# A gated delta-rule block with routed experts: the first stage written out in a fixed order of steps

## The chip, the cores and the metric

The kernel runs on one core of a Trainium2 chip. The metric is device time in microseconds (us). One core has a matrix engine (TensorE, called PE), a vector engine (VectorE, DVE), an activation engine (ScalarE, ACT), a general engine (GpSimd, POOL) and SyncE (SP), whose queue here issues nearly all DMA transfers. Each engine takes its own instructions in the order in which the program has them.

## The reference, cut to what matters

There are two sequences of 2048 tokens with 512 features each. They are normalised and go through 16 heads of a gated delta rule; the first 512 tokens go through 16 experts too (four for each token). All is 32-bit.

```python
xn = layernorm(x)                                   # (2, 2048, 512)
q, k, v = (silu(causal_conv4(xn @ W) + b) for ...)  # 16 heads of 128; k scaled by 128**-0.5
alpha, beta = sigmoid(xn @ Wa + ba), sigmoid(xn @ Wb + bb)
def step(S, (qt, kt, vt, at, bt)):                  # for each token, sequence and head
    err = S @ kt - vt
    S = at * S - bt * outer(err, kt)
    return S, S @ qt
o = layernorm(scan(step)) * ln_w + ln_b
attn = (o * sigmoid(xn @ Wg)) @ Wo
out = x + attn + experts(xn[:512], topk_idx, topk_weight, gate, up, down)
```

## The kernel before, in words

The tokens of a sequence are cut into 16 chunks of 128, four of which make a block of 512. Two heads make a unit; there are 16 units, eight for each sequence. Inside a chunk the recurrence is a set of matmuls with the inverse of a triangular 128x128 matrix; from chunk to chunk a state S is carried. Projections are done transposed (features on partitions, 512 tokens on the free axis), so that the convolution of four taps is three multiply-adds on DVE with shifted slices.

The program has two parts. The **recurrence** (`recurrence`) takes the units one after the other. Its order on PE, DVE, ACT and POOL is written out by hand: generators (`before`, `after`, `output`, `item`, `key_item`, `inverses`, `experts`) yield after each piece, and a loop steps them in turn. While it works on one block it computes the projections of the next block and the keys of the unit two ahead.

The **first stage** prepares what the recurrence needs at its start, and it is what the change touches. Its parts are:

- `norm(b)`, for both sequences: load x, mean and variance (L453, L454), 1/sqrt by a power on POOL (L458), scale (L467), transpose on PE (L473) and evict on ACT (L474), and matmuls with Wa and Wb (L476), 32 columns wide ("gate matmuls" below). Then come the decays: z, exp, log and cumulated sums over a chunk as matmuls with constant triangles (L513), transposed rows written to DRAM (a_d and gin_d). Sequence 0 stays in SBUF as xT; sequence 1 goes to DRAM (xT_d).
- `route`: the experts' lists, that is, which token goes to which tile of which expert (DVE, and small matmuls L938 to L944 and L1002, the latter with "place" matrices).
- `keys(u)` for units 0 and 1, eight pieces each (a block and a head): projection (L155), eviction to raw and cv on ACT (L132, L136), three taps on DVE (L141), SiLU (L146), scores (L205), the decay matrix by a scan on DVE over a row fetched from DRAM (L179 and L196; the row's buffer is single, so the next row is asked for after the scan), and their product (L209). The key, the decay and the product are saved to DRAM.
- `inverses(0)`: the inverses of the 32x32 diagonal blocks of unit 0 on POOL (L264, L267; 30 pairs of steps), written to DRAM as X_d.
- `projection(0)`: q, v and gate of the first block of unit 0, and the loads of its operands.

What sets the order there is a scheduler which takes the program's order and its own estimate of when each instruction is ready. Program order is norm(0), route, and then a loop: the keys of unit 0, all of `inverses(0)`, the keys of unit 1, with steps of norm(1) and of projection(0) put between them. The recurrence starts when all this is written down, and its first instructions can be moved ahead by the scheduler (two of its matmul lines are: L620 and L625 of the first chunk run near 250 us). The tiles of the inverses' operands (`ops` and `invs`) are made and zeroed after the stage.

PSUM banks are in four pools: ps_p (3), ps_l (2), ps_c (2) and ps_o (1).

```python
f0, p0, n1 = firsts(), projection(0), norm(1)
for i, _ in enumerate(f0):
    if i > 12:
        next(n1, None)
    if i in (20, 23, 26, 29):
        next(p0)
drain(n1)
```

Of the kernel before, what the change touches and what calls it, by code (L numbers as in the profile page):

```python
# [1 line left out]

# [5 lines left out]
F32 = mybir.dt.float32  # L8
I32 = mybir.dt.int32
AF = mybir.ActivationFunctionType  # L10
E = mybir.EngineType
# [32 lines left out]
def block_kernel(ctx, tc, x, wq, wk, wv, wg, wo, wa, wb, ba, bb, par, consts,  # L44
# [80 lines left out]
    def conv_taps(ps, p, h0, h, blk):  # L125
# [7 lines left out]
        if blk < NBK - 1:  # L133
            nc.gpsimd.tensor_copy(halo[p][h], raw[:, BLK:])
# [7 lines left out]

    def conv_silu(ps, p, h0, h, blk, dst):
        raw, cv = conv_taps(ps, p, h0, h, blk)
        conv_sum(raw, cv, p, h0 + h)
        nc.scalar.activation(dst, cv, AF.Silu)  # L146
# [73 lines left out]
    def keys(u, xts, bank_k=(ps_p, "p")):  # L220

        b, hp = divmod(u, NP)
        h0 = hp * HG
        begin_keys(u)  # L230
        for blk in range(NBK):
            for h in range(HG):
                ps = proj(wks[u], h, xts(b, blk))
                kt = ap.tile([P, BLK], F32, tag="kf", name="kf", bufs=2)
                conv_silu(ps, 1, h0, h, blk, kt)
                if (blk, h) == (NBK - 1, HG - 1):
                    load_wk(u + 1)
                nc.sync.dma_start(out=k_d[u][blk][h], in_=kt)
                yield
                pk = bank(*bank_k)  # L240
                scores(pk, kt)
                dec = dec_start(u, blk, h)
                tc.keep_in_program_order(dec_run(dec, u, blk, h))
                put_a(pk, dec, u, blk, h)
                yield
# [110 lines left out]
    def item(n, what, h):  # L356
# [20 lines left out]
        raw, cv = conv_taps(ps, p, h0, h, blk)  # L377
# [15 lines left out]
    def key_item(u, blk, h, xts):  # L393
# [15 lines left out]
        raw, cv = conv_taps(ps, 1, h0, h, blk)  # L409
# [19 lines left out]

    with ExitStack() as es:  # L430
        pre = es.enter_context(tc.tile_pool(name="pre", bufs=1))
        cstf = pre.tile([P, N_CONST * P + 1], F32, tag="cst", name="cst")
        nc.sync.dma_start(out=cstf, in_=consts[:, DW:])
        cst = cstf[:, 0:N_CONST * P].rearrange("p (n j) -> p n j", j=P)
# [6 lines left out]
        beta = [pre.tile([P, NC, H], F32, tag=f"beta{b}", name=f"beta{b}") for b in range(NB)]  # L441
        np_ = es.enter_context(tc.tile_pool(name="norm", bufs=2))
        def norm(b):
            psg = bank(ps_o, "o")
            for g in range(NBK):
                xin = [np_.tile([P, HID], F32, tag="xin", name="xin", bufs=4) for _ in range(CB)]
                for i in range(CB):
                    c = g * CB + i
                    nc.sync.dma_start(out=xin[i], in_=x[b, c * C:(c + 1) * C, :])
                mv = np_.tile([P, CB, 2], F32, tag="mv", name="mv")  # L450
                for i in range(CB):
                    st = np_.tile([P, 6], F32, tag="st", name="st")
                    nc.vector.bn_stats(st, xin[i])  # L453
                    nc.vector.bn_aggr(mv[:, i, :], st)  # L454
                ve = np_.tile([P, CB], F32, tag="ve", name="ve")
                nc.vector.tensor_scalar(ve, mv[:, :, 1], EPS, None, ALU.add)
                rs = np_.tile([P, CB], F32, tag="rs", name="rs")
                nc.gpsimd.tensor_tensor(rs, ve, mhalf[:, 0:CB], ALU.pow)  # L458
                if b == 0:
                    xt = xT[b, g] = xp.tile(  # L460
                        [P, NKT, BLK], F32, tag="xT", name=f"xT{b}_{g}", bufs=NBK)
                else:
                    xt = np_.tile([P, NKT, BLK], F32, tag="xt", name="xt", bufs=1)
                for i in range(CB):
# [4 lines left out]
                    if b == 0 and c < FC:  # L469
                        nc.sync.dma_start(out=xn_d[c * C:(c + 1) * C, :], in_=xn)  # L470
# [655 lines left out]
```

## Time and profile before

| | us |
|---|---|
| three runs | 3904.68, 3907.49, 3910.80 (median 3907.49) |
| the profiled execution, device time | 3906.37 |
| its span (first to last instruction) | 3904.3 |
| mean granted clock of TensorE | 0.98 |

| busy in the span | us |
|---|---|
| PE (matmuls; modelled ends) | 3770.2 |
| PEld (weight loads, beside matmuls) | 2461.4 |
| DVE | 2343.6 |
| ACT | 1701.5 |
| POOL | 1682.4 |

A line of the profile's tables of groups and waits names the line of the code, the engine, the tile written and the tiles read. A wait is put down to what released it last. "x8" in a timeline of PE counts records: a 32-bit matmul leaves two, so a projection (four matmuls over the 512 features) is x8. The granted clock is a share of TensorE's full speed.

### The profile page before, as it was taken

The page shows a single profiled execution, that of the slowest core. Times are in us where ns is not written, and L with a number is a line of the kernel's source. Part 1 is how long each engine was busy: PE and PEld are TensorE (multiplying, and loading weights), DVE is VectorE, ACT ScalarE, POOL GpSimd, SP SyncE. Part 2 cuts the span into 40 slices and gives each one's busy share as a digit, 9 for nine tenths or more (in the row PEclk, how much of TensorE's full clock was granted, in tenths as well). Part 3 has the DMA queues.
Part 4 walks back from the last instruction along what each step waited for, and adds up shares of the span by engine and source line. Part 5 has one row for each costly group of instructions (what it writes and reads, how often), then busy time and mean ns, then how long its engine had stood idle before and what let it go on. Part 6 is the DMA issues. An engine that isn't in the chain of part 4 may idle for free.

```text
span 3904.3 us, 59006 instructions
## 1 busy us (share of the span) xinstructions
PE 3770.2 (97%) x18046; PEld 2461.4 (63%) x18046; DVE 2343.6 (60%) x6132; ACT 1701.5 (44%) x4027; POOL 1682.4 (43%) x3046
## 2 busy tenths in 40 slices
PE   7769999999999999999999999999999999998899
PEld 6437767677677766666654466666666666664454
DVE  5536656666666667777750177777777777763231
ACT  3424444444444445555520055555555555542110
POOL 1236546465564636363630053636363545541010
PEclk7789999999999999999999999999999999999999
DMA  4634665655666553545573435353435444342322
GB/s 133 209 98 143 185 169 154 195 158 175 168 176 172 159 178 107 143 132 169 147 240 117 120 103 137 107 139 109 132 111 139 119 127 126 103 111 72 100 75 89
DMA packets 579705, 541.36 MB, mean 139 GB/s; under 512 B 354688, under 2 KB 421760, under 8 KB 574272
## 3 DMA queue, kind: packets, MB, share of 16 engines
q1 hardware_dynamic: 557280, 456.18, 40.6%
q0 software_dynamic: 22112, 81.41, 7.1%
q8 instruction: 147, 2.41, 0.3%
q14 instruction: 166, 1.36, 0.1%
HBM read 363.69 MB, written 173.67 MB: 138 GB/s over the span
## 4 chain that ended last, share of the span: by engine, by line
PE 85%; DVE 6%; DMA 4%; issue 2%; POOL 2%; SPq 1%; ACT 1%; POOLq 0%; DVEq 0%; ACTq 0%
PE p L155 39%; PE p L892 11%; PE p L1044 4%; DVE cv L141 3%; PE o L721 3%; PE l L625 3%; PE p L205 3%; PE o L724 3%; PE c L698 3%; PE c L707 3%; PE c L687 2%; PE p L1059 2%; PE l L640 1%; PE l L658 1%; PE l L667 1%
## 5 line engine op out<-in xcount | busy, mean ns | idle before, releaser
L141 DVE SCALAR_TENSOR_TENSOR cv<-raw,prm,cv 128x512 f32<-128x512 f32 x1152 | 909.5, 790 | 106.2 <-ACT cv L136 44.1
L892 PE MATMUL p<-wo,oTf 128*128 128x512 f32 x1024 | 459.7, 604 | 26.3 <-DMA oTf<-oT_d 25.1
L155 PE MATMUL p<-xT,wq 128*128 128x512 f32 x1024 | 484.6, 596 | 0.0
L653 POOL COPY inv<-iT 32x32 f32<-32x32 f32 x512 | 103.1, 201 | 884.4 <-DVE iT L645 685.1
L155 PE MATMUL p<-xT,wg 128*128 128x512 f32 x1024 | 482.0, 594 | 0.0
L155 PE MATMUL p<-xT,wv 128*128 128x512 f32 x1024 | 481.0, 593 | 0.0
L735 POOL TENSOR_TENSOR rs<-rs,mhalf 128x2 f32<-128x2 f32 x256 | 270.2, 1055 | 485.4 <-DVE rs L734 481.1
L132 ACT COPY raw<-p 128x512 f32<-128x512 f32 x384 | 223.4, 582 | 533.2 <-PE p L155 515.0
L155 PE MATMUL p<-xT,wk 128*128 128x512 f32 x896 | 433.5, 610 | 0.0
L702 ACT COPY w<-c 128x256 f32<-128x256 f32 x256 | 95.3, 372 | 635.0 <-PE c L698 635.0
L714 DVE SCALAR_TENSOR_TENSOR S<-S,gtot,c 128x128 f32<-128x128 f32 x480 | 145.2, 344 | 356.6 <-PE c L707 342.5
L892 PEld LDWEIGHTS p<-wo,oTf 128*128 128x128 f32 x1024 | 193.9, 194 | 252.2 <-issue 223.8
L267 POOL TENSOR_TENSOR Y<-Y,t 128x30 f32<-128x30 f32 (+14 forms) x480 | 308.4, 643 | 37.2
L136 ACT ACTIVATE cv<-p,prm 128x512 f32<-128x512 f32 x384 | 300.4, 782 | 1.7
L264 POOL TENSOR_TENSOR t<-Y 128x30 f32<-128x30 f32 (+14 forms) x480 | 286.2, 596 | 8.8 <-DMA Y<-aT_d 2.3
L155 PEld LDWEIGHTS p<-xT,wq 128*128 128x128 f32 x1024 | 178.0, 192 | 135.8 <-issue 135.8
L155 PEld LDWEIGHTS p<-xT,wg 128*128 128x128 f32 x1024 | 176.8, 191 | 132.3 <-issue 132.1
L155 PEld LDWEIGHTS p<-xT,wv 128*128 128x128 f32 x1024 | 176.3, 191 | 132.0 <-issue 132.0
L691 DVE SCALAR_TENSOR_TENSOR r<-c,gd,kv 128x128 f32<-128x128 f32 x480 | 145.3, 344 | 166.2 <-PE c L687 165.1
L155 PEld LDWEIGHTS p<-xT,wk 128*128 128x128 f32 x896 | 160.6, 198 | 126.3 <-issue 126.3
L388 POOL TENSOR_TENSOR qg<-q,gin 128x512 f32<-128x512 f32 x128 | 194.1, 1516 | 98.6 <-ACT q L386 98.6
L707 PEld LDWEIGHTS c<-w,kg 128*128 128x128 f32 x1024 | 154.1, 191 | 121.4 <-issue 102.1
(172 smaller groups left out, 7145.8 us busy)
## 6 DMA issues: line engine op xcount, KB each, us to landing
row<-a_d SPq DMA_DIRECT2D x128, 258.0 KB
dec_d<-decA SPq DMA_DIRECT2D x128, 258.0 KB
decB<-dec_d SPq DMA_DIRECT2D x64, 516.0 KB
k_d<-kf SPq DMA_DIRECT2D x128, 256.0 KB
k<-k_d SPq DMA_DIRECT2D x64, 512.0 KB
gin<-gin_d SPq DMA_DIRECT2D x128, 256.0 KB
aT_d<-aTf SPq DMA_DIRECT2D x128, 256.0 KB
oT_d<-oT SPq DMA_DIRECT2D x256, 128.0 KB
```

Source lines behind the costliest of these rows:

```text
L132: nc.scalar.copy(raw[:, KS - 1:], ps)
L136: nc.scalar.activation(cv, ps, AF.Identity, bias=cbias(p, h0 + h), scale=tap(p, h0 + h, KS - 1))
L141: nc.vector.scalar_tensor_tensor(cv, raw[:, j:j + BLK], tap(p, h, j), cv, ALU.mult, ALU.add)
L155: nc.tensor.matmul(ps, lhsT=w[:, k, h * D:(h + 1) * D], rhs=xt[k], start=(k == 0), stop=(k == NKT - 1))
L264: nc.gpsimd.tensor_tensor(t, bass.AP(col.tensor, col.offset, [col.ap[0], (Q, j), (0, n)]), bass.AP(row.tensor, row.offset, [row.ap[0], (0, ...
L267: nc.gpsimd.tensor_tensor(Y[:, 0:j, j + 1:], Y[:, 0:j, j + 1:], t, ALU.add)
L388: nc.gpsimd.tensor_tensor(qg[:, h, :], qt[:, h, :], gin, ALU.mult)
L691: nc.vector.scalar_tensor_tensor(r[:, h, :], pq[:, h * D:(h + 1) * D], gd0[b][:, ci, h0 + h:h0 + h + 1], kv[:, 1, h, :], ALU.mult, ALU.add)
L707: nc.tensor.matmul(pss[:, h * D:(h + 1) * D], lhsT=kg[:, h, :], rhs=w[:, h, :], start=True, stop=True)
L735: nc.gpsimd.tensor_tensor(rs, rs, mhalf[:, 0:HG], ALU.pow)
L892: nc.tensor.matmul(py, lhsT=oT[:, h, :], rhs=wos[h], start=(h == 0), stop=(h == H - 1))
L1044: nc.tensor.matmul(ps[:fn, s, :], lhsT=w[f][:, s, k, :], rhs=xt[:, k, :], start=(k == 0), stop=(k == NKT - 1))
```

## The change

It rewrites the first stage as one order written by hand for PE, DVE, ACT and POOL; SP's DMA issues stay with the scheduler.

- `norm` is cut into `fetch`, `moments`, `scaled`, `turned`, `gated` and `decays`. x is loaded into the buffers of q and qg, xn has three buffers instead of two, and the second sequence's transposed chunks go to DRAM in pairs instead of in fours.
- `keys` is gone. The keys use `key_item`, as in the recurrence, which yields after half the projection, after the projection, after the eviction, after the taps and after the SiLU. In slot t the SiLU of key t-2, the taps of key t-1, the projection and eviction of key t, and scores, scan and product of key t-3 are handed out.
- Slots 3 to 10 carry two chunks of the second sequence's norm each. Slots 11 to 18 carry the first block's projections (`item`), the second decays, `route` in steps, and six pairs of steps of `inverses(0)` each. The copies that save the last three columns for the next block (L134) are put off to the end of a slot there.
- `route` counts by one scan along the free axis and three matmuls in place of 32, makes the place matrices in two lots of eight, and yields between its pieces. It moves from before the keys to slots 10 to 18.
- `ops` and `invs` get a pool of their own, and their memsets come first on POOL.
- The recurrence's functions are unchanged; `recurrence(0, p0)` becomes `recurrence(0, ())`.

```diff
-        drain(norm(0))
-        route(nc, bank, ps_l, mp, cst, cstf[:, N_CONST * P:], topk_idx, topk_w, tw, pos, wrow, trow)
...
-        f0, p0, n1 = firsts(), projection(0), norm(1)
-        for i, _ in enumerate(f0):
-            if i > 12:
-                next(n1, None)
-            if i in (20, 23, 26, 29):
-                next(p0)
-        drain(n1)
+        def key_step(i):
+            if 0 <= i < len(keyed):
+                if i not in kgen:
+                    kgen[i] = key_item(*keyed[i], get_xT, later if i >= 8 else None)
+                next(kgen[i], None)
...
+        with tc.manual_schedule(engines={E.PE, E.DVE, E.Activation, E.Pool}):
+            moments(0, 0)
+            for g in range(NBK):
+                if g + 1 < NBK:
+                    moments(0, g + 1)
+                if g + 2 < NBK:
+                    fetch(0, g + 2)
+                for c in range(g * CB, (g + 1) * CB):
+                    scaled(0, c)
+                    turned(0, c)
+                    if c > 0:
+                        gated(0, c - 1)
+                if g > 1:
+                    key_step(g - 2)
+                if 0 < g < 3:
+                    key_step(g - 1), key_step(g - 1)
+            gated(0, NC - 1)
+            d0, d1 = decays(0), decays(1)
+            fetch(1, 0), fetch(1, 1)
+            next(d0)
+            key_step(2), key_step(2)
+            moments(1, 0)
+            next(d0), next(d0)
+            ask(0, 0, 0)
+            key_step(0)
+            next(d0), next(d0)
+            key_step(2)
+            drain(d0)
+            scaled(1, 0), scaled(1, 1)
+            key_step(1), key_step(0)
+            moments(1, 1)
...
+            for t in range(3, len(keyed) + 3):
+                first = t < 11
+                old = t - 3
+                if t == 11:
+                    loads(0)
+                    firsts = [item(0, what, h, later)
+                              for what, h in (("q", 0), ("v", 0), ("q", 1), ("v", 1), ("g", 0), ("g", 1))]
+                if t == 11:
+                    inv = inverses(0)
+                    next(inv)
+                p = firsts[t - 11] if 0 <= t - 11 < 6 else iter(())
+                p1 = firsts[t - 12] if 0 <= t - 12 < 6 else iter(())
+
+                if first:
+                    turned(1, n1)
+                dec = dec_start(*keyed[old])
+                key_step(t - 2)
+                pk = bank(*((ps_l, "l") if old < 8 else (ps_p, "p")))
+                scores(pk, kts.pop(keyed[old]))
+                if first:
+                    gated(1, n1)
+                    turned(1, n1 + 1)
+                else:
+                    next(d1, None)
+                key_step(t), key_step(t)
+                if first:
+                    gated(1, n1 + 1)
+                next(p, None), next(p, None)
+
+                key_step(t - 1)
+                dec_run(dec, *keyed[old])
+                put_a(pk, dec, *keyed[old])
+                key_step(t)
+                next(p1, None), next(p1, None)
+                next(p, None)
+                if first:
+                    n1 += 2
+                    if n1 % CB == 0 and n1 // CB + 1 < NBK:
+                        fetch(1, n1 // CB + 1)
+                        moments(1, n1 // CB + 1)
+                    if n1 < NC:
+                        scaled(1, n1), scaled(1, n1 + 1)
+                if t >= 10:
+                    next(r, None)
+                for _ in range(6):
+                    next(inv, None)
+                next(p1, None)
+                saves()
+            drain(d1, r, inv)
+            load_ops(0)
...
-    recurrence(0, p0)
+    recurrence(0, ())
...
-    for i in range(1, n):
-        nc.tensor.matmul(pr[:, i * NE:n * NE], lhsT=cst[:, K_ONE, :], rhs=sel[:, 0:(n - i) * NE],
-                         start=False, stop=i == n - 1)
...
+    nc.vector.tensor_tensor_scan(cum, goes, sel, 0.0, ALU.mult, ALU.add)
+    run = small("run", NE * n)
+    nc.vector.tensor_tensor(run, cum, sel, ALU.subtract)
+    yield
```

## The prediction

> **What bounds the kernel now.** I read the page first, then the stretches table (busy time by engine between chosen times), then the waits of the stretch that stands out, then its chain. On the page the three rows to read together are PE's total, PE's slices and the granted clock (40 slices of 97.6 us each):
>
> ```profile
> PE 3770.2 (97%) x18046; PEld 2461.4 (63%) x18046; DVE 2343.6 (60%) x6132; ACT 1701.5 (44%) x4027; POOL 1682.4 (43%) x3046
> ...
> PE   7769999999999999999999999999999999998899
> ...
> PEclk7789999999999999999999999999999999999999
> ```
>
> Only the first three slices have a PE below nine tenths and a clock below 0.9. The rest is a TensorE that never stops. The table of stretches (us, then busy us of PE, PEld, DVE, ACT, POOL, then granted clock) puts the border at 288 us:
>
> ```profile
> 0.00:71.00 71.00, 54.30 (x295) 47.65 (x295) 43.97 (x179) 16.59 (x25) 9.71 (x18) 0.81 0.52 159
> 71.00:95.00 24.00, 20.77 (x83) 16.14 (x83) 11.69 (x32) 15.31 (x27) 0.37 (x2) 0.64 0.18 65
> 95.00:155.00 60.00, 46.96 (x220) 36.04 (x220) 35.65 (x65) 25.78 (x52) 5.57 (x11) 0.76 0.67 237
> 155.00:227.00 72.00, 47.88 (x124) 25.27 (x124) 32.05 (x40) 27.43 (x55) 48.39 (x90) 0.83 0.40 114
> 227.00:288.00 61.00, 37.01 (x95) 19.44 (x96) 22.06 (x28) 15.53 (x31) 3.04 (x12) 0.78 0.47 126
> 288.00:3904.00 3616.00, 3563.25 (x17233) 2316.86 (x17231) 2198.22 (x5790) 1600.91 (x3839) 1615.37 (x2914) 1.00 0.48 138
> ```
>
> The last row is the recurrence: PE 98.5% busy at clock 1.00. The five rows above it are the first stage: PE 207 us of 288, much of that at half clock, and DVE only 145. From 155 us on nobody is busy: PE 85 of 133, DVE 54, ACT 43. Who waits for whom before 288 us (total, times, longest):
>
> ```profile
> PE p L205 <- ACT kf L146: 51.2, 12, 13.0
> ...
> DVE cv L141 <- ACT cv L136: 31.6, 12, 6.2
> DVE aTf L209 <- PE p L205: 22.8, 8, 5.0
> DVE decA L196 <- DMA row<-a_d: 20.0, 7, 9.6
> ```
>
> The three engines wait for each other in a ring: projection (PE), evictions (ACT), taps (DVE), SiLU (ACT), scores (PE), product (DVE), one key slot at a time. So the stage is bound by one slot's latency, and it ends on the chain (the chain runs through every piece of 227 to 288 us). Every us taken out there moves the recurrence forward by one, if the recurrence's own order stays. It does: in the built programs PE, DVE, ACT and POOL have the same instructions in the same order from the first projection of the recurrence (PE), its first pT (DVE), its first copy into inv (POOL) to the end; SP's differ only near the border.
>
> **The change, part by part.** I work out when PE is back in its unbroken run, which is at 287.95 us now (first wq matmul of the recurrence in PE's timeline). From there to the end are 3904.3 - 287.95 = 3616.35 us.
>
> *(1) First norm.* PE is busy from 17.9 to the last gate matmul's end at 71.2. In that stretch stood the route's rank and count matmuls (timeline: 1.22+3.84+1.41+1.27+4.28+0.45 = 12.5), the first place matmuls (0.9), two keys' scores (0.94+0.39+2.06 = 3.4) and a first piece of key 2 (2.05). They now come later: 18.8 us off. The memsets of ops and invs (about 7.5 us: 170.7 to 176.6 on POOL now, with their gaps) come to POOL's front, before its first pow near 12 us; they hide behind the load of x, which ends at 10.7. If that cover were gone it would be 2 us. I put the last gate at 71.2 - 18.8 = 52.4, and add 2.6 for order (a group's moments go ahead of the scaling of the group before): 55.
>
> Half clock is what makes this part long. Three stretches show it (PE busy, and the column after POOL is the clock):
>
> ```profile
> 28.00:36.00 8.00, 8.00 (x33) 6.99 (x33) 3.43 (x11) 1.17 (x2) 0.00 (x0) 0.50 0.33 97
> 60.00:76.00 16.00, 16.00 (x57) 12.62 (x57) 10.16 (x34) 5.38 (x7) 4.36 (x4) 0.50 0.58 205
> 124.00:136.00 12.00, 11.67 (x76) 8.96 (x76) 8.64 (x18) 6.32 (x13) 1.74 (x4) 1.00 0.81 283
> ```
>
> PE is busy without a gap at 28 to 36 and 60 to 76 us and stays at 0.50; it is at 1.00 where a 512-column projection came just before. The Trainium skill (TensorE: Matmul & The Clock Gate, section "The HAM clock gate (the 'warmup' mystery)") says that about 3.4 us of sustained matmuls release the clock. By that rule the new dense norm would run warm: four gate matmuls are 0.98 us warm and 1.75 cold, so sixteen chunks would save some 10 us more. The trace speaks against it for such small matmuls, so the sum stays with the cold rows.
>
> *(2) First decays.* From z at 71.2 to the first scan at 95.2 the trace has 24 us. What DVE now has before its first scan: z, az 1.4; four moments 3.6; la, den, reciprocal, beta and copy 3.4; gd, gd1 0.7; two scalings 1.1; four moments 3.6; three keys' taps 3 x 2.25 = 6.7: 20.5, plus some 3 of waits for Exp and Ln (1.28 table and 0.63 each). The transfers (a_d 2.6, row 3.2) lie beside that. First scan at 55 + 24 = **79**.
>
> *(3) Eight slots with the second norm in them.* One slot is: PE two transposed chunks 0.9, two gated 1.6, scores 0.9, projection 3.45 = 6.9 at full clock (12 at half); DVE taps 2.25, scan 1.23, product 0.69, two scalings 1.0 = 5.2, and 3.6 more in two slots; ACT 4.7; the row ring (scan, save, row, scan) 6.0, as between the scans at 95.2, 101.3 and 107.3. None of it waits within its slot, since taps, SiLU and scores belong to three different keys. Floor 6.9; I take 8.5, because PE is sometimes cold. Seven steps, 60 us: scan of key 7 at 139. The same eight keys now take from 95.2 to 175.
>
> *(4) Eight slots with inverses, projections and route.* DVE is the longest queue: route's head 2.9 and slot 11 5.6; slot 12 has decays 3.4, two taps, scan, product, counts 5.5: 15.5; slot 13 12.5; 14 and 15 9.5 each; 16 has taps, scan, product and places 6; then 3.6 and 2. POOL's inverse runs beside it, and a tap then takes 950 ns in the median (182 to 226 us) where it took 747 before 150: nine taps of three, +5.5. The last three slots fall below the row ring and take 6 each: +6. Together **79**, and 4 for waits: the last matmuls of the stage at 139 + 83 = 222. PE has some 58 us there. POOL: Y's load some 8.5 after the last write of unit 0's aT_d, then 45.4 (181.7 to 227.1): X_d goes out near 200, while slots remain; now POOL's idle partners wait for it. SP then issues 44 block loads at 0.45 us, half of them under the last slots, as the row scans wait up to 9.6 us for them at 235.7 now.
>
> The skill (SBUF — State Buffer, section "Who interferes with whom") says that a VectorE instruction with two SBUF inputs and a GpSimd one that reads SBUF exclude each other for a whole instruction. By that, the 33 us of taps and scans beside the inverse would be added in full, some 27 more than my 5.5, and the time would be 3874. The row at hand is 747 to 950, not a doubling, so I keep it.
>
> *(5) The border.* No work of the stage covers the first step of the recurrence any more: PE cold after three thin slots (+3), tokens gathered only after trow (1.05 issue and some 3 landing, of which 3 lie beside matmuls: +1), the first chunk's inputs behind 16 further loads and 8 of Y on SP (about 15 us after the last row, and needed about 15 after): +3. **7**; nothing at best; 20 at worst if that queue is late.
>
> *(6) Route's fewer matmuls* (32 become 3) and the conversion of keys to steps are inside (1) and (4).
>
> Sum: 79 + 60 + 83 + 7 = 229 in place of 287.95, 59 us less. Span 229 + 3616.35 = 3845.4; with the 2.07 that lie around the span of the profiled execution (3906.37 - 3904.3): **3847**. The median of the runs is 1.1 above the profiled one, which I leave.
>
> **The rivals.**
> - *DVE packed solid.* If (1) is warm (-10), (3) runs at its floor (7 x 1.6 = -11) and (4) without waits (-10): 3816. For it: DVE's whole work of the stage is 151 us. Against: the cold rows.
> - *A slot stays a ring.* Three banks of ps_p are shared by scores and two projections, and each engine takes its instructions as written: a late product holds the next scores. If (3) and (4) take 10 and 12.5 a slot: +11 and +17, 3875. For it: from 155 to 280 us eight keys take 15 each now.
> - *Slower.* One mechanism: in slots 11 to 18 bank and row lock the slot into one serial run: cold projections 2 x 5.3, evictions 1.4, three contended taps 3.0 twice, SiLU 0.6, scores 2.1, product 0.7, row 4.1 and scan 1.2: 26.7 us, eight times 214 in place of 83: 3978. It decides from 17.7 us a slot, (287.95 - 7 - 139) / 8. Against: the code staggers those steps over three slots, and even now a key takes 15.
> - *It does nothing.* The order holds for four engines only; SP's loads are still placed by the scheduler, and a held row could give all back: 3907.
>
> **How the numbers follow.** Forecast (3828 to 3862) 0.55; packed 0.17; ring, with partial returns up to 3898, 0.20; nothing 0.03; slower 0.05. What a measurement of this kernel can tell from no change is about 0.2%, 8 us. Faster 0.92, same 0.03, slower 0.05. The bounds of (1) to (5) are 45 to 65, 20 to 28, 42 to 84, 65 to 100 and 0 to 20; not all go one way. Range **3813 to 3884**: below it 0.08, above 0.12.
>
> **What would show it.** First scan near 79 (right if 72 to 88); scans 8 us apart in the first eight and 10 in the others; X_d written near 200; PE unbroken from near 229, clock 1.00 after it, and the recurrence 3616 long. The waits of scores for kf should fall from 51 to below 10. Wrong if scans are over 12 apart, if DVE's largest wait becomes the row, or if the recurrence itself is longer.

## The result, and the profile after

The changed kernel takes 3861.09 us (median of four runs, 3856.55 to 3863.44) beside 3907.44 (3904.68 to 3910.80) for the kernel before: a ratio of 0.9881, with a 95% interval of 0.9866 to 0.9897. The profiled execution took 3863.44 us, its span is 3861.7. So the change gains 46 us where 60 were forecast. The time lies inside the range, and just inside the forecast's own upper end (3862).

The page first: PE's total, its slices and the clock (40 slices of 96.5 us). The first three slices hold 6, 8 and 8 tenths of PE where they held 7, 7 and 6, over a shorter span, and the granted clock reads 0.9, 0.8 and 0.8 there where it read 0.7, 0.7 and 0.8. PE's total is 27 us less, with 58 records fewer and fewer of them cold.

```profile
PE 3743.5 (97%) x17988; PEld 2439.1 (63%) x17988; DVE 2361.5 (61%) x6136; ACT 1700.4 (44%) x4027; POOL 1690.6 (44%) x3046
...
PE   6889999999999999999999999999999999998899
...
PEclk9889999999999999999999999999999999999999
```

Then the stretches, cut at the steps of the prediction (last gate matmul, first scan, scan of key 7, last matmul of the stage, first wq matmul). Columns as before: us, then busy us of PE, PEld, DVE, ACT, POOL, then the granted clock, the DMA share and GB/s.

```profile
0.00:59.00 59.00, 39.60 (x209) 33.49 (x209) 22.19 (x57) 12.86 (x21) 11.37 (x28) 1.00 0.55 171
59.00:79.00 20.00, 14.80 (x50) 8.97 (x50) 19.17 (x42) 12.89 (x23) 3.45 (x5) 0.83 0.30 89
79.00:148.00 69.00, 55.29 (x278) 40.02 (x277) 41.67 (x68) 28.16 (x63) 5.29 (x14) 0.85 0.75 224
148.00:239.00 91.00, 68.96 (x218) 39.00 (x216) 78.95 (x177) 44.28 (x84) 51.87 (x84) 0.85 0.51 150
239.00:242.00 3.00, 1.78 (x7) 1.68 (x8) 1.86 (x4) 0.00 (x0) 0.95 (x1) 0.50 0.45 121
242.00:3861.00 3619.00, 3563.10 (x17233) 2315.98 (x17231) 2197.65 (x5791) 1602.25 (x3838) 1617.65 (x2915) 1.00 0.49 138
```

The last row is the recurrence: 3563.10 us of PE in 17233 records, against 3563.25 in 17233 before. It is the same work, and it begins at 242 instead of 288. The whole gain is in the rows above it. In the fourth row DVE is busy 78.95 of 91 us: in the second eight slots DVE is nearly full (87%), where it was busy for at most 62% of a row of the old stage (43.97 of 71 us).

The waits of this stage (waiting engine and tile, what released it, total us, times, longest us):

```profile
PE c L485 <- DVE xn L465: 30.9, 5, 17.2
...
DVE cv L147 <- ACT cv L142: 16.5, 4, 8.3
...
DVE decA L197 <- DMA row<-a_d: 15.5, 8, 3.8
PE p L156 <- DVE aTf L210: 15.1, 3, 6.5
...
PE p L156 <- DMA wk<-in_wk: 4.6, 1, 4.6
```

PE's largest wait was that of the scores for kf, 51.2 us. It is gone: 0.2 us are left. What PE waits for now is the scaled x (17.2 of the 30.9 us pass before the first chunk is loaded and scaled; the first transpose of the kernel before ran at 17.88), and three times a product of DVE that holds a PSUM bank.

Step by step, in us of the span:

| step of the prediction | predicted | in the profile after |
|---|---|---|
| (1) last gate matmul | 55 | 59.1 |
| (2) first scan | 79 | 78.85 |
| (3) from there to the scan of key 7 | 60 | 69.1 (scan at 147.97) |
| (4) from there to the last matmul of the stage | 83 | 90.9 (238.87) |
| (5) border | 7 | 3.0 to the first wq matmul (241.84), and 3.5 lost just after it |
| span | 3845.4 | 3861.7 |

The 3.5 are the difference between 3861.7 - 241.84 = 3619.9 and the 3616.35 of before: the first wq half is cold (3.53 us where it took 1.88), and the first product with inv waits 1.7 us. The errors of the steps sum to -0.15 + 9.1 + 7.9 - 0.5 = 16.35, which is the whole difference of the spans.

### The profile page after: what moved, and what is told of

It is laid out like the page before. It is cut to its first block, busy times and chain, and to the rows that moved or that the text cites. A ratio compares the mean times of both kernels' runs of the same rounds, so it can differ in the third digit from the quotient of the medians.

```text
span 3861.7 us, 58910 instructions
## 1 busy us (share of the span) xinstructions
PE 3743.5 (97%) x17988; PEld 2439.1 (63%) x17988; DVE 2361.5 (61%) x6136; ACT 1700.4 (44%) x4027; POOL 1690.6 (44%) x3046
## 4 chain that ended last, share of the span: by engine, by line
PE 84%; DVE 5%; DMA 2%; issue 1%; POOL 1%; ACT 1%; SPq 1%; POOLq 0%; ACTq 0%; DVEq 0%
PE p L156 39%; PE p L987 11%; PE p L1154 4%; DVE cv L147 3%; PE o L816 3%; PE l L720 3%; PE o L819 3%; PE c L793 3%; PE c L802 3%; PE p L206 3%; PE c L782 2%; PE p L1169 2%; PE l L735 1%; PE l L753 1%; PE l L762 1%
## 5 line engine op out<-in xcount | busy, mean ns | idle before, releaser
L134 ACT COPY raw<-p 128x512 f32<-128x512 f32 x384 | 223.7, 583 | 525.1 <-PE p L156 510.6
```

What stands on the lines that cost most here:

```text
L134: nc.scalar.copy(raw[:, KS - 1:], ps)
```

## The experiments

Two theories were to be told apart for the 16 us. **Neighbour:** the second slots are bound by DVE, whose instructions POOL's inverse stretches, and the small dependent operations of the route more than the taps. **Ring:** a slot is held by single buffers (the row, the weights, a bank) and by the order in which DVE takes its work. Later a third came up, **the inverse's own chain**: product, write, load, 30 pairs on POOL, write, load.

How sharp is a measurement? The run x0_control is the changed kernel once more. Its profile has the first wq matmul at 236.55, where the first profile has 241.84. The recurrence's second sequence (from its first output projection to the end, the same instructions in each kernel) took 1903.0 us in the profile of before, 1901.3 in that of after, and 1900.6 to 1911.5 in the others. From the first wq matmul to the end it is 3616.35 us in the profile of before, 3619.9 in that of after, and 3616.5 to 3629.0 in the others, so what is gained at the border does not always arrive whole at the end. So differences below 5 us, in one profile or between medians, are not read as effects here. The runs were made on four chips, and each ratio is to the kernel before as it was measured beside the run.

### x0_control

No edit.

> The changed kernel again, word for word, so that the others are read against it on the same chip: 0.987 to 0.989 of the kernel before, and the first matmul of the recurrence (wq) within 4 us of 241.8.

3858.02 us (before 3903.53), ratio 0.9891 (0.9874 to 0.9909). Scans at 76.78 to 144.94 for the first eight and to 233.36 for the rest. The first wq matmul is 5.3 us from that of the first profile, where 4 were allowed. It is the yardstick for the runs below: 68.2 us for step (3), 88.4 to the last scan.

### x1_no_inverse_steps

```diff
-        for j in range(1, Q - 1):
+        for j in range(1, Q - 1 if u else 1):
```

The kernel leaves out the 30 pairs of steps of unit 0's inverse on POOL, so that this unit's X is not an inverse. Everything else runs.

> Leaves out the 30 pairs of multiply and add by which POOL inverts the diagonal blocks of unit 0 (the load of Y, the set of the diagonal, the copy to X and the writes of X_d stay), so unit 0's inverse is not computed. Theory A (POOL stretches DVE in slots 11 to 18): there the places, counts and comparisons of route took 5.24, 6.68 and 5.37 us in the changed kernel against 3.2, 3.9 and 2.7 worked out from before, taps up to 3.58 against 2.25 and one scan 2.97 against 1.23; all of that goes, so the last eight slots shrink by 11 to 16 us and the kernel takes 3846 to 3851. Rival B (DVE is slow there by its own queue of small dependent operations, or the slots wait for PE's banks): the small operations keep their durations and the time stays within 4 us of 3861.

3850.98 us (before 3902.90), ratio 0.9864 (0.9847 to 0.9880); first wq matmul at 224.88. The groups of DVE's three small chains of the route, in the stretch from 80 to 245 us (shapes, count, then busy us, mean ns of one, and idle before them), first after, then x1:

```profile
L1076 DVE SCALAR_TENSOR_TENSOR te<-cst,ends,te 128x31 f32<-128x31 f32 x16 | 6.2, 385 | 0.6
L1090 DVE TENSOR_SCALAR ge<-first,posf 128x32 f32<-128x32 f32 x16 | 5.4, 413 | 0.0
L1052 DVE SCALAR_TENSOR_TENSOR tiles<-cnt,tiles 128x16 f32<-128x16 f32 x16 | 4.7, 295 | 0.6
```

```profile
L1076 DVE SCALAR_TENSOR_TENSOR te<-cst,ends,te 128x31 f32<-128x31 f32 x16 | 4.0, 251 | 0.6
L1052 DVE SCALAR_TENSOR_TENSOR tiles<-cnt,tiles 128x16 f32<-128x16 f32 x16 | 3.9, 246 | 0.5
L1090 DVE TENSOR_SCALAR ge<-first,posf 128x32 f32<-128x32 f32 x16 | 3.5, 296 | 0.0
```

Together 16.3 against 11.4 us. The taps' mean is 856 ns between 148 and 239 us after the change, and 750 there in x1. From the scan of key 7 to the end of the last stage matmul DVE is busy 67.8 us of 79.4 in x1 and 78.5 of 88.5 in the control: 10.7 us less DVE work and a stretch 9.1 us shorter, where theory A had 11 to 16. The neighbour is real and is worth about 9 us at this place. The time of the whole kernel does not show it by itself, because x1 takes the inverse's chain away too; the stretch and the durations do.

### x2_route_early

```diff
-                pk = bank(*((ps_l, "l") if old < 8 else (ps_p, "p")))
+                pk = bank(ps_p, "p")
...
-                if t >= 10:
-                    next(r, None)
+                next(r, None)
```

The route goes to slots 3 to 11, ahead of the inverse.

> Moves route from slots 10 to 18 to slots 3 to 11 (the scores of all slots take their bank from ps_p, so that route may hold ps_l). In slots 3 to 10 DVE was idle for some 20 of 69 us and POOL did next to nothing. Theory A (place matters: idle time and a quiet POOL are in the early slots): route's 22 us cost 8 to 12 there, and the late slots lose 28: 3842 to 3852. Rival B (the early slots are a chain through DVE too, and route just moves): what the late slots lose the early ones gain, 3857 to 3863.

3861.57 us (before 3902.90), ratio 0.9890 (0.9874 to 0.9907): no gain. Yet what the neighbour theory says of DVE happened, in the same view:

```profile
L1075 DVE SCALAR_TENSOR_TENSOR te<-cst,ends,te 128x31 f32<-128x31 f32 x16 | 4.0, 251 | 0.6
L1051 DVE SCALAR_TENSOR_TENSOR tiles<-cnt,tiles 128x16 f32<-128x16 f32 x16 | 2.8, 175 | 0.6
L1089 DVE TENSOR_SCALAR ge<-first,posf 128x32 f32<-128x32 f32 x16 | 2.4, 236 | 0.0
```

9.2 us for the three chains, near the 9.8 worked out from before, and 2.2 less than in x1: the pairs of the inverse are not all that stretched them. The first eight slots did not get longer for it (scans from 77.80 to 146.50). The stage's last matmuls, the scores of the last key, end at 218, where the last stage matmul of the changed kernel ends at 238.87 and that of the control at 233.5. So rival B's time came, but not for its reason. And then PE stands still (its timeline: start, us, operation, idle before it and who ended that):

```profile
216.84 1.16 PE L206 MATMUL p<-kf 128*128 128x128 f32 x8 [1.47 <-ACT kf L396]
236.27 0.61 PE L714 MATMUL l<-ilo,a 128*128 128x32 f32 x2 [18.28 <-DMA ihi<-X_d]
```

The 18.28 us are spent on blocks of the inverse, whose write was issued at 215.82. So the relief of DVE is hidden under a second bound that ends at nearly the same time: the inverse itself. In the changed kernel it shows as a mere 1.3 us, since DVE is as late as the inverse.

### x3_second_key_weights and x4_scale_before_moments

In the first slots' row of the stretches, PE is busy 55.29 of 69 us. Its idle time there is 4.6 us for wk of the second unit, which is loaded into the buffer of the first, and 9.1 for xn where a group's moments stand ahead of a scaling on DVE. Each of these stops is followed by cold matmuls (start, us):

```profile
119.60 3.60 PE L156 MATMUL p<-xT,wk 128*128 128x512 f32 x8
...
131.25 6.00 PE L156 MATMUL p<-xT,wk 128*128 128x512 f32 x8 [4.55 <-DMA wk<-in_wk]
...
140.60 3.60 PE L156 MATMUL p<-xT,wk 128*128 128x512 f32 x8
...
147.54 2.74 PE L156 MATMUL p<-xT,wk 128*128 128x512 f32 x6
```

From 140.60 to 147.54 a slot runs without a stop and takes 6.9 us on PE, the floor of the prediction; the one that ends in the wait for wk takes 11.7. Two runs try to take one stop away each.

```diff
         begin_keys(0)
+        wks[1] = load_w(ap, "X", wk, HG, "wk1")
```

> Key weights of unit 1 are loaded at the start into the buffer of X (which is written only at the end of the inverse), in place of one buffer of weights that is reloaded after the last key of unit 0. The changed kernel shows PE waiting 4.55 us for that load, and a cold projection of 6.00 after it in place of 3.60. Theory A: the wait lay on the chain of slots, DVE waited 8.3 us for the taps' input behind it: 5 to 9 us less, 3852 to 3856. Rival B (the row ring or DVE's queue was due at the same time): 0 to 2 less, 3859 to 3861.

3855.68 us (before 3902.90), ratio 0.9877 (0.9860 to 0.9893); key 7's scan at 143.36. The wait for wk is gone. The time lies in theory A's range, but the ratio is not told from the control's.

```diff
+                    if n1 < NC:
+                        scaled(1, n1), scaled(1, n1 + 1)
                     if n1 % CB == 0 and n1 // CB + 1 < NBK:
                         fetch(1, n1 // CB + 1)
                         moments(1, n1 // CB + 1)
-                    if n1 < NC:
-                        scaled(1, n1), scaled(1, n1 + 1)
```

> In the slots of the second norm where a group's moments stand ahead of the scaling of the next two chunks (two slots), scaling goes first. PE waited 5.6 and 3.5 us for that scaling at 94 and 115 us, and ran cold after it. Theory A (PE's transposes wait for DVE's order): 5 to 8 us less, 3853 to 3856. Rival B (those slots last as long as their row takes, some 10 us, whatever PE does): within 3 of 3861.

3858.82 us (before 3902.90), ratio 0.9885 (0.9869 to 0.9902); key 7's scan at 144.00. This edit did not take its stop away: PE still waits 6.8 us for xn in these slots (1.3, 4.1 and 1.4), against 7.5 in the control (4.9 and 2.6), and DVE's wait for the row grew from 14.0 to 22.3. Both scans stand within 1.6 us of the control's 144.94; counted from the first scan, step (3) takes 64.7 us in x3 and 65.9 in x4 against 68.2, less than the 5 us that are read as an effect. What x3 took out came back as next to nothing at the scans.

### x5_two_rows

```diff
-            rows[u, blk, h] = row = ap.tile([P, CB * DW], F32, tag="row", name="row")
+            rows[u, blk, h] = row = ap.tile([P, CB * DW], F32, tag="row", name="row", bufs=2)
...
-        m = blk * HG + h + 1
+        m = blk * HG + h + 2
```

Beside it the place matrices come in lots of four, to make room for the second row.

> Two buffers for the decay rows, each asked for one key further ahead; to make room the place matrices come in four lots of four. Theory A (early slots last 9.9 us because a scan waits for a row that could only be asked for after the scan before it, behind other issues of SP: 15.5 us of waits): scans of the first eight keys come 8 to 9 us apart, the first wq 6 to 12 us earlier, the time 6 to 12 below the control. Rival B (the slots of the second norm are as long as PE, DVE and ACT make them by waiting for one another): the wait moves to another releaser, 0 to 3 below the control.

3860.73 us (before 3903.53), ratio 0.9889 (0.9872 to 0.9905). DVE's wait for the row, 15.5 us in the profile after, is gone from the list, and the time has not moved. The waits for x's load (10.4 in the profile after, 15.1 here) and for ACT's cv (16.5, here 20.1) have grown in its place. That is how a ring would look: of three waits that end within a few us of each other, taking one away shows the next.

### x8_three_edits and x9_three_edits_two_rows

x8 is x2, x3 and x4 in one kernel; x9 adds the second row.

> Route in the early slots, own buffer for unit 1's key weights, and scaling ahead of moments, together. Alone, the first of them left PE waiting 18.3 us at the border for ihi from X_d. Theory A (with DVE relieved, POOL's chain from unit 0's last product over Y, 30 pairs and X_d to the operands sets the border; the other two edits bring its start forward by some 14): first wq at 222 to 228, the time 10 to 16 below the control. Rival B (that wait is the queue of SP at the border, which comes when slots end early): first wq at 233 to 238 as with route alone.

> The three edits and two buffers for rows. If the start of the inverse is what counts and rows hold the early slots, a further 4 to 9 us below the three edits; if rows are not what holds them, the same as the three edits within 2.

x8: 3859.74 us, ratio 0.9884 (0.9867 to 0.9900). x9: 3859.19, ratio 0.9888 (0.9871 to 0.9904); before 3903.53 for both. Neither differs from the control. In x9 PE has finished the keys near 216 and waits 16.3 us for top<-X_d, the inverse's block; in x8 it waits 18.6 us for bot<-X_d. X_d is issued at 214 in both. In x8 5.5 us pass from there (214.35) to the issue of the first load (219.84), 13.6 until the sixteenth has been issued on SP's queue (233.41), and 1.6 until PE starts (235.01). So the queue at the border, which rival B names, is a part of it, and the inverse's late end is the other. All four edits of the slots end against this chain.

### x6_before_new_route

The kernel before, with the new way to count alone (one scan and three matmuls, at the route's old place ahead of the keys).

```diff
-    nc.tensor.matmul(pr[:, 0:n * NE], lhsT=cst[:, K_LT, :], rhs=sel, start=True, stop=False)
-    for i in range(1, n):
-        nc.tensor.matmul(pr[:, i * NE:n * NE], lhsT=cst[:, K_ONE, :], rhs=sel[:, 0:(n - i) * NE],
-                         start=False, stop=i == n - 1)
+    nc.vector.tensor_tensor_scan(cum, goes, sel, 0.0, ALU.mult, ALU.add)
...
+    nc.tensor.matmul(pr[:, 0:NE * n], lhsT=cst[:, K_LT, :], rhs=sel, start=True, stop=False)
+    nc.tensor.matmul(pr[:, 0:NE * n], lhsT=cst[:, K_ONE, :], rhs=run, start=False, stop=True)
```

> The kernel before with one part of the change alone: the experts' lists by one scan and three matmuls in place of 32, still ahead of the keys. Theory A (PE's work in the first norm is on the path, as step (1) of the prediction counted it): the rank and count matmuls shrink from 12.5 us of PE to some 1.5, and the first scan and the recurrence's first wq matmul come 8 to 12 us earlier: 3891 to 3899 beside a before of 3903. Rival B (before's key slots are a ring whose length the route's work does not touch, and its matmuls lie in DVE's or ACT's waits): the gain at the front is eaten by the new scan and DVE's work on it, and the time stays within 4 us of before.

3900.19 us (before 3905.47), ratio 0.9985 (0.9976 to 0.9994). The first scan comes at 83.43 instead of 95.23, and the first wq matmul at 275.53 instead of 287.95: 12 us at both places, so the slots of before keep their length in sum and nothing of it is eaten on the way. Of the 16.4 us that the first scan gains in the changed kernel, 11.8 are to be had from this part alone. The medians show 5.3 us (2 to 9); of the rest some 5 are lost between the first wq matmul and the end in this profile (3622.7 after it, against 3616.35), and how much of that is chance these runs do not tell.

### x7_inverse_unsplit

```diff
-                for _ in range(6):
-                    next(inv, None)
+                for _ in inv:
+                    pass
```

> The changed kernel with the 30 pairs of steps of the inverse handed to POOL in one piece at slot 11 in place of six pairs a slot. POOL's small copies of the last three columns for later keys (halo) then stand behind the whole inverse. Theory A (the split is worth its trouble): the taps of the keys of slots 12 and later wait for a halo copy until the inverse ends, near 161 + 48 = 209, and five slots of 7 to 8 us follow: first wq matmul near 250 to 262, 15 to 25 us after the changed kernel's, so 3872 to 3885. Rival B (DVE's queue sets the slots, and a wait of the taps for POOL fills only time that DVE would spend stretched): within 5 us of the changed kernel, 3853 to 3865.

3876.96 us (before 3905.47), ratio 0.9922 (0.9909 to 0.9936); first wq matmul at 256.10: theory A's numbers. POOL's last pair and the copies behind it, and then what DVE did:

```profile
200.67 0.26 POOL L249 TENSOR_TENSOR Y<-Y,t 128x30 f32<-128x30 f32 x1
200.86 0.15 POOL L253 MEMSET Y<- 128x32 f32 x1
201.08 1.89 POOL L255 COPY X<-Y 128x1024 f32<-128x1024 f32 x1
202.92 0.31 POOL L589 COPY halo<-raw 128x3 f32<-128x3 f32 x2
```

```profile
179.39 0.06 DVE L534 MEMSET rt<- 128x2 f32 x1
203.39 3.35 DVE L147 SCALAR_TENSOR_TENSOR cv<-raw,prm,cv 128x512 f32<-128x512 f32 x3 [23.94 <-POOL raw L131]
```

DVE stands still for 23.94 us behind a copy of three columns. So handing the inverse out in sixes is worth 12 to 16 us to the change (the ratio beside those of the control and of the first measurement). The same trace gives the inverse's price with the engine to itself: its pairs run from 162.94 to 200.93, 38.0 us. In the changed kernel they run from 163.13 to 223.49, 60.4 us. Between them stand 11.3 us of other work on POOL (small copies, two products of 512 columns, three gathers of the experts' weights) and 6.7 us in which POOL stands still (4.45 ahead of the first gather, 2.26 for the taps); that leaves some 42 for the pairs. Splitting keeps the copies moving, and it makes the inverse late.

### x10_border_queues and x12_inverse_chain

x10 is x9, and the writes of the inverse are issued by POOL, the first 16 block loads by ACT and POOL.

```diff
-            nc.sync.dma_start(out=X_d[u][s].rearrange("h g c e -> (h g c) e"),
+            (nc.sync if u else nc.gpsimd).dma_start(out=X_d[u][s].rearrange("h g c e -> (h g c) e"),
...
+            eng = nc.sync if n else (nc.scalar, nc.gpsimd)[h]
...
-                nc.sync.dma_start(out=op["ilo"][row:row + Q], in_=block(0, lo))
+                eng.dma_start(out=op["ilo"][row:row + Q], in_=block(0, lo))
```

> The four edits together (route in slots 3 to 11, second unit's wk in a buffer of its own, scaling ahead of the moments, two row buffers) and, new, the two writes of the inverse issued by POOL and the 16 block loads of the first operands by ACT and POOL in place of SP. Theory A (after these edits PE waits 16.3 us for block loads because they stand on SP's queue behind the saves and rows of the last two keys): that wait falls below 9 us, the first wq matmul comes at 224 to 229 in place of 233.7, and the time is 5 to 9 us under the changed kernel's, 3849 to 3854, ratio .986 to .9875. Rival B (the loads land late because the DMA engines are busy with 128-byte packets of the writes, or POOL issues slowly): the wait moves to another of the same tiles or to the gathered tokens, and the time stays within 3 us of the changed kernel, ratio .988 to .9895.

3854.27 us (before 3905.47), ratio 0.9866 (0.9851 to 0.9881). The ratio is the one that theory A named. The cause is not shown, for PE still waits 14.4 us at the border where 9 were the limit, and the first wq matmul stands at 234.75. On POOL's timeline:

```profile
215.88 1.95 POOL L255 COPY X<-Y 128x1024 f32<-128x1024 f32 x1
218.12 0.61 POOL L257 DMA_DIRECT2D X_d<-X  x1 [0.30 <-POOL X L255]
...
225.77 0.61 POOL L315 DMA_DIRECT2D ihi<-X_d  x1 [5.10 <-DMA X_d<-Y]
```

POOL's own queue is free, and it waits 5.10 us for the write to land; then come eight issues of 0.55 us. So SP's queue was not the only thing between the inverse and its use; the round trip through DRAM is another. In the changed kernel, where SP issues both, the first load of this kind is issued 2.9 us after the write (223.60 and 226.50), and here 7.0 (218.74 and 225.77). Whether POOL's issue makes it slower, which rival B allows for, these runs do not settle.

x12 is x10 with the front of the same chain on POOL's queue: the writes of unit 0's last two products, the eight loads of Y, and Y's write ahead of the copy into X.

```diff
-        nc.sync.dma_start(out=aT_d[u][:, o:o + CB, :], in_=aT)
+        (nc.sync if u or blk < NBK - 1 else nc.gpsimd).dma_start(out=aT_d[u][:, o:o + CB, :], in_=aT)
...
-                nc.sync.dma_start(
+                (nc.sync if u else nc.gpsimd).dma_start(
                     out=Y[o:o + NC], in_=aT_d[u][g * Q:(g + 1) * Q, h * NC:(h + 1) * NC,
```

> The kernel of x10 with the rest of the inverse's chain off SP's queue: the writes of the last two products of unit 0 and the eight loads of Y are issued by POOL (in x10 the last of these writes was issued at 152.36, 4 us and more after its product, and the last Y load at 157.98), and Y is written to DRAM ahead of its transposed copy X. Theory A (after the other edits the chain product, Y, inverse, X_d, block loads sets the start of the recurrence by itself, for PE stands idle 14.4 us before the first chunk of it): the inverse starts 4 to 6 us earlier, X_d is written 5 to 8 us earlier, and the first wq matmul comes near 227 to 230 in place of 234.75; 3846 to 3851 beside a before of 3905, ratio .985 to .986. Rival B (the halo copies that POOL makes for the taps of slots 11 and 12 now stand behind POOL's waits for the products' landing, so DVE's slots move out by what the chain gains): last scan after 225 in place of 220, first wq matmul at 233 or later, and the time within 3 us of x10's ratio, .9857 to .9875.

3857.59 us (before 3905.51), ratio 0.9880 (0.9864 to 0.9897). Theory A's numbers did not come, and of rival B's only one: the first wq matmul stands at 238.34 (233 or later). DVE's slots did not move out (last scan at 221.74, against 220.05), so the halo copies were not the trouble. But the inverse did not start earlier either:

```profile
148.49 0.59 POOL L213 DMA_DIRECT2D aT_d<-aTf  x1 [1.42 <-DVE aTf L210]
...
155.27 1.73 POOL L1125 DMA_INDIRECT w<-in_ew,wrow  x1 [1.65 <-DMA aT_d<-aTf]
156.99 2.55 POOL L239 DMA_DIRECT2D Y<-aT_d  x4
165.85 0.72 POOL L248 TENSOR_TENSOR t<-Y 128x30 f32<-128x30 f32 x1 [6.31 <-DMA Y<-aT_d]
```

The product's write is issued 4 us earlier than on SP's queue, takes 6 us to land, the loads stand behind a gather and take 6 us more. The start at 165.85 is 1.8 us later than in x10 (164.10). Of x10's and x12's results the cautious reading is that neither is told from the control: their intervals overlap with its own. The best median of a kernel that computes everything is x10's.

## Why the prediction was right, and which terms were off

**The mechanism is right in the main.** The scores waited for kf, one slot at a time. In the staggered slots that wait falls from 51.2 to 0.2 us, the sixteen scans come in 160 us where they took 182 (95.2 to 277.1), and the recurrence is the same work 46 us earlier. The forecast was its own most likely case; the range and the sign held. The time lies only 0.9 us inside the forecast's upper end, though, and the two large terms, (3) and (4), missed in the same direction. Where the 46 us lie is best counted by products, the last step of a key (us):

| | before | after | x6 (before, new route) | x7 (after, inverse in one piece) |
|---|---|---|---|---|
| start of the first product | 96.8 | 80.2 | 85.2 | 79.7 |
| from there to the product of key 7 | 76.6 | 69.1 | 75.3 | 69.3 |
| from there to the last product | 106.6 | 90.7 | 106.8 | 105.3 |
| from there to the first wq matmul | 7.9 | 1.9 | 8.2 | 1.9 |

So 16.6 us were gained ahead of the first product, 7.5 in the first eight keys, 15.9 in the second eight and 6.1 at the border. Of the 16.6, x6 gets 11.7 by the new way to count alone. The 15.9 hang on the inverse being handed out in pieces: in x7, staggered but with the inverse in one piece, the second eight keys take 105.3 us, about as long as before. No run staggers the slots and changes nothing else, so what the staggering is worth by itself is argued from the waits and not shown.

The prediction's "from 95.2 to 175" for the first eight keys of before runs from a scan to a product (173.4). The scan of key 7 ran at 160.35, so from scan to scan these keys took 65.1 us before and 69.1 after: by the measure of (3) they did not get shorter. And one sign of being wrong did show: four times two scans are over 12 us apart (13.5, 16.6, 16.9 and 14.5), though the means are 9.9 and 11.3.

**(1) and (2): two errors that cancel, by luck.** The last gate matmul is 4.1 us late and the decays are 4.3 us quicker. The 12.5 us for the route's matmuls were taken off a stretch that begins at 17.9, but 5.06 of them ran ahead of it, and the transposes of after begin only 0.7 us earlier, which about makes the 4.1 (start, us; before, then after):

```profile
13.19 1.22 PE L938 MATMUL l<-sel,cst 128*128 128x256 f32 x2 [13.19 <-DVE sel L936]
14.20 3.84 PE L940 MATMUL l<-sel,cst 128*128 128x240 f32 x18
17.88 1.04 PE L473 MATMUL c<-unit,xn 128*128 128x128 f32 x8
```

```profile
17.15 1.97 PE L485 MATMUL c<-unit,xn 128*128 128x128 f32 x8 [17.15 <-DVE xn L465]
```

The first scaling stands behind the second group's moments now (16.56 on DVE, 13.26 before). In x6, which keeps the old program but for the count, the transposes begin at 14.31, the last gate matmul is 7.6 us earlier and the first scan 11.8. The clock was not the error: in the sum, which kept the rows of before, the gate matmuls of 6 of the 16 chunks are cold, and after the change those of 7 are. The rows of after, from the first norm (start, us):

```profile
35.37 1.09 PE L485 MATMUL c<-unit,xn 128*128 128x128 f32 x4
36.25 1.75 PE L493 MATMUL o<-wab,xT 128*128 128x32 f32 x8
37.82 6.62 PE L156 MATMUL p<-xT,wk 128*128 128x512 f32 x8
44.28 0.60 PE L485 MATMUL c<-unit,xn 128*128 128x128 f32 x4
44.72 0.98 PE L493 MATMUL o<-wab,xT 128*128 128x32 f32 x8
```

Ten us of PE without a gap, from 28 to 37.8, stayed at half speed (four gate matmuls 1.75), and after one projection of 512 columns the same four took 0.98. That is what the prediction read from the rows of before, and the rule of the Trainium skill (TensorE: Matmul & The Clock Gate, section "The HAM clock gate (the 'warmup' mystery)") did not hold for these small matmuls. The later chunks ran warm, since keys are projected among them.

**(3) is the term of 60 us, and it measured 69.** It stood on a slot of 8.5 with PE "sometimes cold". A warm slot without a stop takes 6.9. Three stops on PE stand in the stretch: 4.6 us for the second unit's wk, which the prediction does not name, and 9.1 for xn in the two slots with moments, which it had counted as DVE work and not as a wait of PE. Two of them are followed by a cold projection (6.00 and 4.88 where 3.60 is warm). That these stops are where the 9 us sit is read from the trace and not shown by a run: x3 removed one and brought 1.6 us at the scan of key 7, and x4 did not remove its own. So the term is a ring of waits, as the rival "a slot stays a ring" has it, and at its price (9.9 us a slot, the rival's 10), but the waits are for weights and for DVE's order and not for the banks that the rival names.

**(4) is the term of 83, and it measured 91.** Its list holds 72.6 us of DVE work and 10 of waits; DVE was busy 78.95 us and idle 12, so it is the work that was priced too low. Taps were stretched less than the prediction put it: 30 by 856 - 750 ns is 3.2 us, where 5.5 were allowed. The step that failed is the price of the route's small operations, which was taken from undisturbed rows: 3.2 + 3.9 + 2.7 = 9.8 us, measured 16.3. x1 shows most of the cause: without POOL's inverse these take 11.4 us, and DVE's work in this stretch falls by 10.7. Small operations and taps leave some 2 us of the 6.3 unassigned. The second rule of the Trainium skill that was weighed (SBUF — State Buffer, section "Who interferes with whom") is right in that a neighbour costs. Its whole price, 27 us more than the 5.5, is not what the runs show: about 5 more.

**The inverse was costed as work beside the path, and it is a second bound.** 45.4 us after a start 8.5 us behind the last write were assumed, with X_d out near 200. It started 13 us behind the product's end, took 60.4 (x7: because it is split, above all), and X_d was written from 223.6. The loads of Y stood in SP's queue:

```profile
152.76 1.05 SPq L213 DMA_DIRECT2D aT_d<-aTf  x1
153.86 7.14 SPq L237 DMA_DIRECT2D Y<-aT_d  x5
161.10 0.44 SPq L397 DMA_DIRECT2D k_d<-kf  x1
```

It did not move this result by itself, since DVE was as late. It is where the gain of x2, x8 and x9, which all freed DVE, was lost: PE waits 16 to 19 us for its blocks there. The chain that ended last in before already ran through these loads (on SP's queue between 226.90 and 249.08, then 1.81 us for ilo<-X_d to land), so by that view the inverse was not beside the path even then.

**(5) is right in its sum** (6.5 for 7), in part by other terms: a cold first wq half costs 1.65 us where 3 were put, the gathered tokens 0.3 where 1 was, the first block of the inverse 1.3 and the first inv 1.7, and the rest is matmuls of the first chunk, which before ran inside the stage (near 250). Its bound of 20 for a late queue was not needed here, and is about what x2, x8 and x9 paid (16 to 19 us).

**The rivals.** A slot that stays a ring gave the price of (3), but not of (4): 91 us over eight slots is 11.4, and the time it named (3875) is 14 above the result. Its mechanism shows in (4) all the same: three times a projection waits for a bank that a late product of DVE holds, 15.1 us in all. The serial slots did not come: no slot is over 17 us. The packed stage failed at (3) and at the inverse. What is open: why x3 gives back less than the stop it removes, what holds xn in x4, and whether x10 is faster than the changed kernel.

## What to carry to other kernels

When a stage that waited in a ring is staggered, price the new slots by rows that were measured with the same neighbours beside them: the chains of small operations on DVE grow most (9.8 to 16.3 us here) when POOL works next to them. Follow also the longest chain that was taken for work beside the path, with its DRAM round trips and its place in the queue, to the moment at which it is needed; here it ended within a few us of the new critical engine, so four edits of the slots showed no gain, alone or together. And work that is handed to an engine in pieces is worth its trouble only for what queues behind it: 12 to 16 us here for copies of three columns, at the price of a piecewise work that ends 22 us later.

## What the runs showed of the hardware that was not expected

- A row of the granted clock can be at odds with the matmuls. From 28 to 37 us the profile after gives PE 1.00 in the clock's column, and the gate matmuls take 1.75 us, as they do where it gives 0.50. The durations were taken.
- From the issue of a 512 KB write of the inverse (Y) to the issue of the first load that had to wait for it, SP's queue took 2.6 to 2.9 us in x0, x7 and the changed kernel, 5.5 in x2 and x8 and 8.5 in x9, with whatever else stood in it. Where POOL issued the two writes it took 4.9 to 8.1 us (x10 and x12). Taking the chain off SP's queue did not shorten it.
- An issue of a plain DMA took 0.55 to 0.61 us on POOL, 0.31 to 0.45 on ACT and mostly 0.30 to 0.54 on SP (x10); a gather on POOL took 1.0 to 1.9 (x10, x12 and the changed kernel).
- The neighbour's cost is uneven. Beside POOL's inverse a DVE operation on 512 columns took 856 ns for 750 (1.14 times), and one on 16 to 32 columns 295 to 413 ns where it took 175 to 251 with the route moved away from the inverse (1.5 to 1.75 times), and 246 to 296 at the same place without the inverse's pairs (x1). POOL's own pairs took some 42 us for 38.0.
